# One tile of a block taken from a table held on chip by 0/1 products, in two of three blocks of the first layer and one of four of the second

## The chip, the cores and the metric

The kernel runs on one core of a Trainium2 chip. The metric is the device time of that core in microseconds (us), as the median of several runs. A difference of about 0.2% is what a measurement of this kernel can tell from no change.

## The reference

Two layers of a graph network run one after the other over 6250 nodes with 128 features and 200,000 edges, which are sorted by the node that they end at (`dst`). Cut to what matters:

```python
h = maximum(layernorm(x), 0)                       # layer 0: attention with 8 heads
z = (h @ W).reshape(N, 8, 16)
el, er = einsum(z, attn_l), einsum(z, attn_r)      # (N, 8) each
e = leaky_relu(el[src] + er[dst], 0.2)
a = exp(e - segment_max(e, dst)[dst])
agg = segment_sum(z[src] * a[:, :, None], dst)
x = x + agg / maximum(segment_sum(a, dst), 1e-9) + bias

h = maximum(layernorm(x), 0)                       # layer 1: tensor product messages
s, v = h[:, :32] @ W_up_s / sqrt(32), (h[:, 32:] by 3) @ W_up_v / sqrt(32)
w0, w1, w2, w3 = split(silu(silu(f8 @ A1 + b1) @ A2 + b2) @ A3, 4)
msg = [s[src]*y_s*w0, dot(v[src], y_v)/sqrt(3)*w3, s[src]*y_v*w1, v[src]*y_s*w2]   # 256 per edge
x = x + (segment_sum(msg, dst) / 10) @ W_out / sqrt(64)
```

All of it is in float32. What matters here is `z[src]` with `el[src]` in layer 0, and `s[src]`, `v[src]` in layer 1: for each of the 200,000 edges a row of a table is fetched, 136 floats wide in layer 0 and 128 in layer 1.

## The kernel before, in words

The edges are cut into 1563 tiles of 128 edges, one edge to a partition. 16 tiles (`KB`) make a block; there are 98 blocks (`NB`). The inputs are such that a block's edges end within 128 nodes of a window that moves on by 64 nodes from block to block (a check at the start takes another path otherwise). The nodes stand in 50 tiles of 128 (`NX`).

A first stage computes the table of layer 0 and writes it to HBM as `ft0` (in the profile `ft`). Then layer 0 goes through the blocks, and while it does so it writes the rows of the table of layer 1, `ft1` (also `ft` in the profile), as nodes become complete. Layer 1 then goes through the blocks again.

**Where the rows come from.** Most tiles are gathered: `gather` (L833) issues one indirect DMA from GpSimd (POOL) for each tile, 128 rows each, into a column of the block's tile `g`. `z_pool` holds five such tiles `g`, and `take_rows` asks for a block's rows some blocks ahead, so POOL waits only for a free `g`. In every third block (`by_row`, 31 blocks) the last tile is fetched in another way: `rows_by_row` issues 128 single-row DMAs from SyncE (SP), at L1130, to a tile `r`, with the row numbers read into registers at L1126, 32 at a time; `filled` copies `r` into `g` on ScalarE. `rows_until` spreads these row DMAs between SP's other work, some three blocks ahead of their use. The first 24 tiles of layer 1 are gathered from `ft1z`, a copy of the table in which the last three node tiles are zero, so that they can start before layer 0 ends; `late_ends` and `late_rows` add the missing rows by products.

**Layer 0**, one iteration of the loop for each block `c`, written out by hand in order for TensorE, VectorE, ScalarE and SP. `logits` (L1228) adds the gathered `el` and the `er` of the block, and TensorE transposes the sum (L1231). `ends_of` builds the 0/1 matrices `s` of the block after next (L1149); `masks_of` (L1193), `turned` (L1203, the 0/1 matrices transposed on TensorE into the bank `p_d`, of which there are two, and evicted by ScalarE) and `er_of` (L1214) prepare the next block; `maxima`, `neighbours`, `weights` finish the softmax of the block before (`exp` at L1270, and its transpose at L1271); `weighted` (L1281) scales the rows, and `sums` (L1286) adds them up by products with `s`. Each second block completes a node tile: `node_x` to `node_s` compute its `x` and its row of the next table, and `node_out` has SP write it to `ft1` and `ft1z` (L1350). `x` of all nodes stays on chip in `fx_all`. The gathers of the next blocks run beside all this on POOL.

**Layer 1**, four tiles at a time: `network` (L1568, L1572) computes the edge network of the next block, `tensor_weights` (L1585) its last product, `messages` (L1605 to L1614) multiplies on VectorE, `one_hot` (L1149) builds the 0/1 matrix, `sums1` (L1622) adds up. `node1` multiplies with `W_out` and `node_out1` writes the result (L1642). `edge_rows` has SP load a block's edge inputs (L1549, L1551).

Of the kernel before, what the change touches and what calls it, by code (L numbers as in the profile page):

```python
# [18 lines left out]
P = 128  # L19
# [722 lines left out]
def tile_even_edges(  # L742
# [88 lines left out]
    def gather(to, table, tiles, width, first=0):  # L831
        for k, t in enumerate(tiles, first):
            nc.gpsimd.indirect_dma_start(  # L833
                out=to[:, k, :width], out_offset=None, in_=table,
                in_offset=bass.IndirectOffsetOnAxis(ap=src_col[:, t : t + 1], axis=0))
        return to
# [171 lines left out]
def even_edges(tc, v):  # L1008
# [8 lines left out]
    with ExitStack() as ctx:  # L1017
        z_pool = ctx.enter_context(tc.tile_pool(name="fz", bufs=5))
        const = ctx.enter_context(tc.tile_pool(name="fconst", bufs=1))
        s_pool = ctx.enter_context(tc.tile_pool(name="fs", bufs=16))  # L1020
        row_pool = ctx.enter_context(tc.tile_pool(name="frow", bufs=3))
        of_l0 = ctx.enter_context(ExitStack())
        l0c = of_l0.enter_context(tc.tile_pool(name="l0c", bufs=1))
# [15 lines left out]
        x_all = const.tile([P, NX, P], F32, name="fx_all")  # L1039
# [3 lines left out]
        identb = l0c.tile([P, P], BF, name="fidentb")  # L1043
        nc.vector.tensor_copy(identb, ident)
# [50 lines left out]
        a3p = const.tile([P, 2, P], F32, name="fa3p")  # L1095
        nc.sync.dma_start(a3p, v["a3p"])
# [4 lines left out]
        wout = const.tile([P, 2, P], F32, name="fwout")  # L1101
        nc.sync.dma_start(wout, v["wout"])
# [5 lines left out]
        with tc.tile_pool(name="fat_ps", bufs=1, space=PSUM) as at_ps:  # L1108
            col = l0c.tile([P, P], F32, name="fcol")
# [36 lines left out]
        def one_hot(t, m, iota=iota):  # L1146

            s = s_pool.tile([P, 4, P], F32, name="s")
# [17 lines left out]

        sv_late = const.tile([P, NL, P], F32, name="fsv_late")
# [4 lines left out]
        with tc.manual_schedule(engines=in_order), \  # L1172
                tc.tile_pool(name="l0", bufs=2) as l0, \
                tc.tile_pool(name="l0n", bufs=2) as l0n, \
                tc.tile_pool(name="l0_ps", bufs=1, space=PSUM) as l0_ps:
# [5 lines left out]
            nc.scalar.copy(iota_p, iota)  # L1181

# [15 lines left out]
            def turned(c, q):  # L1198
                if 4 * q < c["kt"]:
                    m = min(4, c["kt"] - 4 * q)  # L1200
                    p_d = l0_ps.tile([P, 4, P], F32, name="p_d", bufs=2)
# [87 lines left out]

            def node_rows(i, n):  # L1290
                nc.sync.dma_start(x_all[:, i : i + n, :],
                                  xp[i * P : (i + n) * P].rearrange("(j p) f -> p j f", p=P))

            def with_bias(i, n):
                x_i = x_all[:, i : i + n, :]
                nc.vector.tensor_add(x_i, x_i, bias_b[:, None, :].to_broadcast([P, n, F]))

            def node_x(u):
                i, n, agg = u["i"], u["n"], u["agg"]
                x_i = x_all[:, i : i + n, :]  # L1300
# [14 lines left out]
            def node_h(u):  # L1315
                i, n = u["i"], u["n"]
                rs, mr = normal(l0n, u["mv"], u["rs"], n, f"n{n}")
                xn = u["xn"] = l0n.tile([P, 2, P], F32, name="xn")
                nc.scalar.activation(xn[:, 0, :], x_all[:, i, :], AF.Identity, bias=mr[:, 0, :],
                                     scale=rs[:, 0, :])  # L1320
                if n == 2:
                    nc.vector.tensor_scalar(xn[:, 1, :], x_all[:, i + 1, :], u["mv"][:, 1, 0:1],
# [20 lines left out]
            def node_out(u):  # L1343
                i, n, sv = u["i"], u["n"], u["sv"]
                first = i * P - W0
                for table in (t1, t1z) if i < LATE else (t1,):
                    if i == 0:
                        nc.sync.dma_start(table[: P - W0, :], sv[W0:, 0, :])
                    else:
                        nc.sync.dma_start(  # L1350
                            table[first : first + n * P].rearrange("(j p) f -> p j f", p=P), sv)

# [12 lines left out]
            def take_rows(g):  # L1365
                if 0 < g < NG:
                    c = cs[g]
                    t = c["b"] * KB + c["o"]
                    c["z"] = gathered(t0, range(t, t + c["kt"] - (c["b"] in by_row)), ZW)
# [42 lines left out]
            rows, rows_until.n, late = rows_by_row(0, t0, ZW), 0, []  # L1412
            for i in range(2):
                node_rows(i, 1)
            for g in range(NG - 3):
# [3 lines left out]
                for n in late:  # L1419
                    node_out(n)  # L1420
                if g % 2 == 0 and g // 2 + 2 < NX - 2:
# [6 lines left out]
                logits(c)  # L1428
                ends_of(n2, 0)
# [3 lines left out]
                maxima(c)  # L1433
                ends_of(n2, 1)
# [5 lines left out]
                er_of(n1, 0)  # L1440
                if b4:
                    weights(b4)
                for n in nodes:
# [3 lines left out]
                if b4:  # L1447
                    bank_of(b4)
                    weighted(b4, 0)
                turned(n1, 3)  # L1450
                er_of(n1, 2)
                if b4:
                    weighted(b4, 8)
                for n in nodes:
# [4 lines left out]
                if b4:  # L1459
                    sums(b4, 0)  # L1460
                for n in nodes:
# [6 lines left out]
                late = nodes  # L1468
                if b4:
                    sums(b4, 8)  # L1470
                if g == NG - 4:
# [8 lines left out]
            for n in late:  # L1480
                node_out(n)
            with_bias(NX - 2, 2)
# [5 lines left out]
            maxima(c3)  # L1488
            neighbours(c4, c5, c3)
# [26 lines left out]
            (u,) = ended(c4, st)  # L1516
            weighted(c2, 0)
# [22 lines left out]
        with tc.manual_schedule(engines=in_order), \  # L1540
                tc.tile_pool(name="l1", bufs=3) as l1, \
                tc.tile_pool(name="l1n", bufs=2) as l1n, \
                tc.tile_pool(name="l1_ps", bufs=2, space=PSUM) as l1_ps:

# [8 lines left out]
            def network(b, step):  # L1553
# [7 lines left out]
                if step == 3 or 2 * q0 + 8 >= KT[b] and second:  # L1561
                    c["yp"] = held[:, P + b % 3 * KB * 3 : P + (b % 3 + 1) * KB * 3].rearrange(
# [61 lines left out]

            def node1(i, agg):
                x_i = x_all[:, i, :]
                p_n = l1_ps.tile([P, 4, P], F32, name="p_n", bufs=1)
# [3 lines left out]
                nc.scalar.copy(m_t, p_n[:, :2])  # L1631
                for q in range(2):
                    nc.tensor.matmul(p_n[:, 2, :], m_t[:, q, :], wout[:, q, :], start=q == 0, stop=q == 1)
                nc.vector.scalar_tensor_tensor(x_i, p_n[:, 2, :], POST, x_i, op0=OP.mult, op1=OP.add)
                return i

            def node_out1(i):
                x_i = x_all[:, i, :]
                if i == 0:
                    nc.sync.dma_start(out[: P - W0, :], x_all[W0:, 0, :])  # L1640
# [5 lines left out]
            iota_p = held[:, :P]  # L1646
# [25 lines left out]
            def late_rows(t):  # L1672
                if t < NE:
                    z, k0, oh = blk[t // KB]["z"], t % KB, late_ends.of.pop(t)
                    p_n = l1_ps.tile([P, 4, P], F32, name="p_n", bufs=1)
# [224 lines left out]
```

## Time and profile before

| what | value |
|---|---|
| median of 3 runs | 3866.83 us (3866.21 to 3874.36) |
| the profiled execution's own time | 3867.01 us |
| its span in the profile | 3865.1 us |
| POOL busy | 2900.2 us (75%), of it 3024 gathers at L833 2857.7 us |
| PE (matmul) busy | 2825.6 us (73%) |
| DVE (VectorE) busy | 2237.5 us (58%) |
| ACT (ScalarE) busy | 1403.0 us (36%) |
| mean granted TensorE clock | 0.813 |

The profile tells each engine's busy time; a group of instructions has its line, engine, operation, output and input, count, busy time, mean ns of one, and the idle time of its engine before it with what ended it. A float32 product is two instructions on TensorE. The granted clock (PEclk) is the share of full speed at which TensorE runs. Layer 0's loop lasts from about 60 us to about 1960 us of the span, and layer 1's from there to the end.

### The profile page before, as it was taken

What the parts mean: (1) busy time and instruction counts of PE and PEld (TensorE: products, weight loads), DVE (VectorE), ACT (ScalarE), POOL (GpSimd) and SP (SyncE); (2) the same over time, 40 slices, a digit from 0 to 9 for tenths busy, and PEclk for the clock granted to TensorE, in tenths of its full rate; (3) what the DMA queues carried; (4) which work ended last, traced back from release to release, by engine and by line L of the source; (5) the groups of instructions that cost most, each with busy time, mean ns of one, the idle gap of its engine ahead of it and who ended that gap; (6) DMA issues with size and microseconds to landing.
All of it is one profiled execution on the core that took longest, in us unless ns stands there. A gap on an engine that the chain in (4) does not pass through costs nothing. (4 is left out here: it accounts for less than half of the span.)

```text
span 3865.1 us, 62861 instructions
## 1 busy us (share of the span) xinstructions
PE 2825.6 (73%) x14836; PEld 2380.3 (62%) x14836; DVE 2237.5 (58%) x5485; ACT 1403.0 (36%) x3625; POOL 2900.2 (75%) x3074
## 2 busy tenths in 40 slices
PE   4666566666666666666688888888887788888777
PEld 3666566666566656656576666666665666666655
DVE  6555444444444444444457777777766666666666
ACT  3333322232323233322324444444444444444443
POOL 6777777777777777777777777777777777777776
PEclk7676666666666666666689999999999999999999
DMA  6222222222222222222222222222222222222221
GB/s 176 60 64 62 65 64 62 65 64 63 63 64 63 64 62 65 62 64 62 62 60 62 62 62 62 62 63 62 61 63 62 62 62 62 62 61 62 61 61 50
DMA packets 192048, 250.91 MB, mean 65 GB/s; under 512 B 78768, under 2 KB 141872, under 8 KB 191664
## 3 DMA queue, kind: packets, MB, share of 16 engines
q0 software_dynamic: 98048, 207.21, 22.6%
q1 hardware_dynamic: 93184, 39.50, 3.9%
q8 instruction: 120, 1.97, 0.2%
q14 instruction: 264, 2.16, 0.2%
q10 hardware_dynamic: 432, 0.08, 0.0%
HBM read 232.98 MB, written 13.25 MB: 64 GB/s over the span
## 5 line engine op out<-in xcount | busy, mean ns | idle before, releaser
L833 POOL DMA_INDIRECT g<-ft,fsrc x3024 | 2857.7, 945 | 934.4 <-issue 859.1
L1622 PE MATMUL p_u<-mj,s 128*128 128x256 f32 x3126 | 793.6, 398 | 211.2 <-DVE mj L1614 209.8
L1622 PEld LDWEIGHTS p_u<-mj,s 128*128 128x128 f32 x3126 | 591.1, 196 | 379.4 <-DVE mj L1614 303.3
L1286 PE MATMUL p_u<-g,s 128*128 128x136 f32 x3062 | 588.1, 372 | 1.0 <-DVE g L1281 0.4
L1286 PEld LDWEIGHTS p_u<-g,s 128*128 128x128 f32 x3062 | 563.2, 276 | 1.7 <-DVE g L1281 1.6
L1589 ACT ACTIVATE p_w<-p_w,yb 128x64 f32<-128x64 f32 x1563 | 450.3, 288 | 120.5 <-PE p_w L1585 78.8
L1605 DVE TENSOR_TENSOR vy<-g,p_i 128x384 f32<-128x384 f32 x387 | 213.0, 550 | 364.6 <-DMA g<-ft,fsrc 258.1
L1585 PE MATMUL p_w<-fa3p,h 128*128 128x256 f32 x1564 | 412.3, 387 | 0.0
L1203 PE MATMUL p_d<-fident,s 128*128 128x128 f32 x1563 | 370.6, 400 | 0.9 <-DVE s L1149 0.9
L1585 PEld LDWEIGHTS p_w<-fa3p,h 128*128 128x128 f32 x1564 | 289.3, 195 | 117.9 <-issue 51.9
L1228 DVE TENSOR_TENSOR e_s<-g,p_n 128x128 f32<-128x128 f32 x96 | 27.5, 286 | 554.6 <-DMA g<-ft,fsrc 498.1
L1570 ACT ACTIVATE h<-p_h,fb 128x512 f32<-128x512 f32 x196 | 134.7, 687 | 580.2 <-PE p_h L1568 580.2
L1203 PEld LDWEIGHTS p_d<-fident,s 128*128 128x128 f32 x1563 | 300.7, 218 | 11.6 <-DVE s L1149 1.1
L1196 ACT COPY mk<-p_m 128x385 f32<-128x385 f32 (+1 forms) x99 | 47.7, 482 | 701.4 <-PE p_m L1193 693.6
L1281 DVE TENSOR_TENSOR g<-g,pe 128x1024 f32<-128x1024 f32 x193 | 225.5, 1209 | 127.3 <-ACT g L1272 127.3
L1205 ACT CAST d<-p_d 128x512 bf16<-128x512 f32 x391 | 228.2, 586 | 180.4 <-PE p_d L1203 137.2
L1231 PE MATMUL pe<-fident,e_s 128*128 128x128 f32 x98 | 37.7, 384 | 329.9 <-DVE e_s L1229 329.9
L1149 DVE TENSOR_TENSOR s<-p_n,fdloc 128x512 f32<-128x512 f32 x391 | 266.1, 682 | 7.2 <-ACT sv L1341 3.4
L1149 DVE TENSOR_TENSOR s<-p_i,fdloc 128x512 f32<-128x512 f32 x391 | 266.4, 681 | 3.8 <-ACT p_i L1564 3.8
L1568 PE MATMUL p_h<-ft,fa1p 128*128 128x128 f32 x1568 | 215.4, 282 | 67.7 <-DMA ft<-in_e_f_dram 67.7
L1568 PEld LDWEIGHTS p_h<-ft,fa1p 128*128 128x128 f32 x1568 | 209.2, 196 | 88.6 <-issue 72.4
L1575 ACT ACTIVATE h<-p_h,fb 128x512 f32<-128x512 f32 x196 | 134.7, 687 | 304.4 <-PE p_h L1572 304.4
(213 smaller groups left out, 3345.6 us busy)
## 6 DMA issues: line engine op xcount, KB each, us to landing
r<-ft SPq DMA_DIRECT2D x3968, 0.5 KB
r<-ft SPq DMA_DIRECT2D x3968, 0.5 KB
g<-ft,fsrc POOLq DMA_INDIRECT x3024
ft<-in_e_f_dram SPq DMA_DIRECT2D x98, 64.0 KB
yb<-in_e_y_dram SPq DMA_DIRECT2D x98, 32.0 KB
fx_all<-in_e_xp_dram SPq DMA_DIRECT2D x48, 64.0 KB
out_dram<-fx_all SPq DMA_DIRECT2D x47, 64.0 KB
ft<-sv SPq DMA_DIRECT2D x46, 64.0 KB
```

The source lines that it names most:

```text
L833: nc.gpsimd.indirect_dma_start(out=to[:, k, :width], out_offset=None, in_=table, in_offset=bass.IndirectOffsetOnAxis(ap=src_col[:, t : t + ...
L1149: nc.vector.tensor_tensor(s[:, :m], iota[:, None, :].to_broadcast([P, m, P]), dloc[:, t : t + m].unsqueeze(2).to_broadcast([P, m, P]), OP. ...
L1203: nc.tensor.transpose(p_d[:, k, :], c["s"][q][:, k, :], ident)
L1205: nc.scalar.copy(d[:, :m], p_d[:, :m])
L1281: nc.vector.tensor_mul(zh, zh, p_a[:, k0 : k0 + m].unsqueeze(3).to_broadcast([P, m, H, D]))
L1286: nc.tensor.matmul(c["p_u"][:, :ZW], c["s"][k // 4][:, k % 4, :], c["z"][:, k, :], start=c["o"] + k == 0, stop=c["o"] + k == KT[c["b"]] - 1)
L1568: nc.tensor.matmul(p_h[:, q, :], a1p[:, q0 + q, :], c["ft"], start=True, stop=True)
L1570: nc.scalar.activation(c["h1"], p_h, AF.Silu, bias=b1)
L1585: nc.tensor.matmul(w[:, k : k + n].rearrange("p k a u -> p (k a u)"), c["h2"][q // 4][:, q % 4, :], a3p[:, :n].rearrange("p k f -> p (k f) ...
L1589: nc.scalar.activation(w[:, k, ::2, :], w[:, k, ::2, :], AF.Copy, scale=c["yb"][:, k0 + k, 0:1])
L1605: nc.vector.tensor_mul(vy, v_n, y_p)
L1622: nc.tensor.matmul(blk[b]["p_u"][:, :MW], u["s"][:, k, :], u["mj"][:, k, :], start=k0 + k == 0, stop=k0 + k == KT[b] - 1)
```

## The change

In 48 blocks of layer 0 (set `dense`: from block 21 to 93, those not in `by_row`) and in 21 blocks of layer 1 (`dense1`: every fourth from block 10), one tile of the block (`KD`, the last but one) is no longer gathered. Its rows come from products with the whole table, which is held on chip as the sum of three bfloat16 parts (`t0s`, `t1s`; `in_three` splits a float32 into them).

The 50 node tiles are taken in three ranges of 17, 17 and 16, so one 0/1 matrix of 128 by 128 serves three node tiles at once. For a tile of edges, `spread` (`dense_ends` in layer 1) turns its 128 node numbers, reduced to a place within their range (`key`), into a row on every partition by one product; `ends_to` compares it with the places of 17 node tiles, in two VectorE instructions, to 17 bfloat16 0/1 matrices; `rows_of` (`dense_rows`) makes 17 times 3 bfloat16 products, each 408 columns wide in layer 0 and 384 in layer 1, that add up in one bank `p_x`; and `taken` (`dense_taken`) picks of the three ranges the right one with `part`, in three VectorE instructions, into `g`.

In layer 0 the table is read back from HBM in the first 17 iterations (`asked`, one SP transfer of three node tiles) and split (`split`). In layer 1 the parts come ready: layer 0 splits each node tile of the new table (`parts`) and writes `x` and the parts together to a new HBM tensor `fx1` (`parts_out`, one SP transfer of 128 by 320 floats a node tile), and layer 1 loads them in its first eight blocks (`table_tiles`). `x` no longer stays on chip: layer 1 reads it back from `fx1` (`node_rows1`), one transfer a node tile. To make room in PSUM, `p_d` has one bank where it had two (the other is `p_x`). The weights `fa3p` and `fwout` are loaded where layer 1 begins, not in the setup; the order on SP there is: the write of the last but two node tiles' table rows, their `x`, `fa3p`, `fwout`, five loads of edge inputs, then the write of the last two tiles' table rows.

The counts on the engines as the built programs have them: POOL's gathers go from 1516 to 1468 in layer 0 and from 1508 to 1487 in layer 1 (from `ft1`); TensorE gets 3519 products and as many weight loads of the new kind, and 69 spreads; SP gets 47 writes of `fx1` with parts and 2 without, 49 reads of `x` from it, 8 loads of `t1s` and 18 reads of the table.

```diff
         def gather(to, table, tiles, width, first=0):
-        for k, t in enumerate(tiles, first):
+        for t in tiles:
+            k = first + t - tiles[0]
...
+        NR = -(-NX // 3)
+        KD = KB - 2
+        order = sorted(range(NR), key=lambda k: (k > 0, 2 * NR + k < NX, k))
+        half = (NR + 1) // 2
+        TS = 3
+        dense = {b for b in range(-(-NX // TS) + 4, NB - 4) if b not in by_row}
+        dense1 = set(range(10, NB - 4, 4))
...
+        def in_three(to, of, rest):
+            to = [to[..., k, :] for k in range(3)]
+            nc.vector.tensor_copy(to[0], of)
+            nc.vector.tensor_sub(rest, of, to[0])
+            nc.vector.tensor_copy(to[1], rest)
+            nc.vector.tensor_sub(to[2], rest, to[1])
...
+            def spread(c, pe):
+                b = c["b"]
+                c["at"] = pe[:, 2 * P : 3 * P]
+                nc.tensor.matmul(c["at"], ranges[0][:, b : b + 1].to_broadcast([P, P]), ident,
+                                 start=True, stop=True)
+            def ends_to(c, h):
+                n = half if h == 0 else NR - half
+                oh = c["oh", h] = ohs[:, h * half : (h + 1) * half, :]
+                nc.vector.tensor_tensor(
+                    oh[:, :n], c["at"].unsqueeze(1).to_broadcast([P, n, P]),
+                    ranges[2][:, h * half : h * half + n].unsqueeze(2).to_broadcast([P, n, P]), OP.is_equal)
+            def rows_of(c, k0, n):
+                if k0 == 0:
+                    p_x = l0_ps.tile([P, 512], F32, name="p_x")
+                    c["p_x"] = p_x[:, : 3 * ZW].rearrange("p (r f) -> p r f", f=ZW)
+                for k in range(k0, min(k0 + n, NR)):
+                    i = order[k]
+                    m = len(range(i, NX, NR))
+                    for s in range(3):
+                        nc.tensor.matmul(c["p_x"][:, :m, :], c["oh", k // half][:, k % half, :],
+                                         t0s[:, i::NR, s, :], start=k == 0 and s == 0,
+                                         stop=k == NR - 1 and s == 2)
+            def taken(c):
+                b, z, part = c["b"], c["z"][:, KD, :], ranges[1]
+                nc.vector.tensor_scalar(z, c["p_x"][:, 0, :], part[:, b, 0:1], None, op0=OP.mult)
+                for r in (1, 2):
+                    nc.vector.scalar_tensor_tensor(z, c["p_x"][:, r, :], part[:, b, r : r + 1], z,
+                                                   op0=OP.mult, op1=OP.add)
...
-                    p_d = l0_ps.tile([P, 4, P], F32, name="p_d", bufs=2)
+                    p_d = l0_ps.tile([P, 4, P], F32, name="p_d")
...
-                    c["z"] = gathered(t0, range(t, t + c["kt"] - (c["b"] in by_row)), ZW)
+                    c["z"] = gathered(t0, [k for k in range(t, t + c["kt"])
+                                           if not (c["b"] in by_row and k % KB == KB - 1)
+                                           and not (c["b"] in dense and k % KB == KD)], ZW)
...
                 logits(c)
+                to, was = n2["b"] in dense, n1["b"] in dense
+                if to:
+                    spread(n2, c["pe"])
                 ends_of(n2, 0)
                 if n1 is not none:
                     masks_of(n1)
                 turned(n1, 0)
                 maxima(c)
+                if to:
+                    ends_to(n2, 0)
+                if was:
+                    rows_of(n1, half, 4)
+                for n in late:
+                    parts(n)
                 ends_of(n2, 1)
...
                 er_of(n1, 0)
+                if was:
+                    rows_of(n1, half + 4, NR)
                 if b4:
                     weights(b4)
+                if was:
+                    taken(n1)
...
                     weighted(b4, 0)
+                if to:
+                    ends_to(n2, 1)
                 turned(n1, 3)
                 er_of(n1, 2)
                 if b4:
                     weighted(b4, 8)
+                if to:
+                    rows_of(n2, 0, 3)
...
                     sums(b4, 0)
+                if to:
+                    rows_of(n2, 3, 3)
...
                     sums(b4, 8)
+                if to:
+                    rows_of(n2, 6, half - 6)
+                split(g - 3)
...
+            def dense_step(b, q):
+                if b + 1 in dense1:
+                    if q == 1:
+                        dense_ends(b + 1)
+                    elif q > 1:
+                        dense_rows(b + 1, (q - 2) * 4, 4)
+                if b in dense1:
+                    dense_rows(b, 8 + 3 * q, 3)
+                    if q == 2:
+                        dense_taken(b)
```

## The prediction

> **What bounds the kernel now.** I read the busy row of the page, then the groups, the chain of waits, the windows by stage, and the timeline of single iterations. First POOL:
>
> ```profile
> L833 POOL DMA_INDIRECT g<-ft,fsrc x3024 | 2857.7, 945 | 934.4 <-issue 859.1
> POOL g L833 <- issue: 861.0, 2823, 0.3
> DVE e_s L1228 <- DMA g<-ft,fsrc: 500.2, 81, 12.0
> DVE vy L1605 <- DMA g<-ft,fsrc: 258.1, 159, 3.7
> ...
> 1200.00:1700.00 500.00, 332.58 (x1959) 304.91 (x1960) 231.25 (x505) 153.16 (x347) 377.90 (x401) 0.65 0.28 63
> 2200.00:2700.00 500.00, 418.47 (x1925) 330.98 (x1926) 355.41 (x907) 219.24 (x617) 377.99 (x401) 0.97 0.24 62
> ```
>
> The first row gives 75% busy, but the idle time before a gather is 0.30 us each and called issue: POOL waits for nobody. 401 gathers in 500 us, in both layers: one per 1.249 us (0.945 plus 0.30), from 60 us to the end. VectorE waits for landed rows in both layers. So the time is the number of gathers times 1.249 us plus a head and a tail, as long as the other engines keep pace. The two window rows (columns: length, PE, PEld, DVE, ACT, POOL busy, clock, DMA) show what room they have: PE 66% at a granted clock of 0.65 in layer 0, 84% at 0.97 in layer 1.
>
> One iteration of layer 0, and what the clock does in it:
>
> ```profile
> 1220.05 0.29 DVE L1228 TENSOR_TENSOR e_s<-g,p_n 128x128 f32<-128x128 f32 x1 [4.58 <-DMA g<-ft,fsrc]
> 1227.24 0.47 PE L1271 MATMUL pe<-fident,a 128*128 128x128 f32 x1 [2.25 <-ACT a L1270]
> 1230.47 5.55 PE L1286 MATMUL p_u<-g,s 128*128 128x136 f32 x32
> 1239.66 0.29 DVE L1228 TENSOR_TENSOR e_s<-g,p_n 128x128 f32<-128x128 f32 x1 [7.27 <-DMA g<-ft,fsrc]
> ...
> 1232.00:1233.00 1.00, 1.00 (x6) 1.00 (x6) 0.40 (x1) 0.00 (x0) 0.81 (x1) 0.50 0.29 72
> 1234.00:1235.00 1.00, 1.00 (x11) 1.00 (x10) 0.00 (x0) 0.00 (x0) 0.69 (x2) 1.00 0.30 66
> 1241.00:1242.00 1.00, 1.00 (x7) 1.00 (x6) 0.97 (x3) 0.48 (x1) 0.69 (x2) 0.50 0.31 72
> ```
>
> It starts when rows land (1220.05), PE ends it at 1236.0, and the next rows come at 1239.66: 16.0 us of work in a period of 19.6. An iteration with a node tile (1201.07 to 1217.9) takes 16.9. The clock is 0.50 through most of it, becomes 1.00 after 3 us of unbroken sums, and falls back after the idle stretch.
>
> The queue next to its limit is SP's:
>
> ```profile
> 1217.51 0.42 SPq L1291 DMA_DIRECT2D fx_all<-in_e_xp_dram  x1
> 1218.03 34.57 SPq L1130 DMA_DIRECT2D r<-ft  x84
> ```
>
> A row DMA comes each 0.32 us, and 32 of them need a register load of 2.17 us (L1126). A third of 128 rows a block is 42.7 x 0.32 = 13.7 us, loads 1.33 x 2.23 = 3.0, the node transfers (0.43 + 0.47 + 0.50)/2 = 0.7: 17.4 us of 19.6.
>
> **The change, part by part.** *Gathers removed.* 48 in layer 0 and 21 in layer 1: 69 x 1.249 = 86.2 us less on POOL. Three blocks of layer 0 took 47 gathers = 58.7 us and will take 45 = 56.2; four of layer 1 went from 78.1 to 76.9. This is the whole gain; the rest asks whether the others keep this pace.
>
> *TensorE in layer 0.* No product like the new ones is in the loop. The nearest rows: four bf16 products of the setup (L923, three of 512 columns) start 0.215 us apart at full clock, 0.42 ns a column, so 408 columns take 0.171 us, and 0.34 at half clock (the 385-column L1193 there keeps PE 0.32). Their weight load (bf16, L1214: 0.18 us for four at full clock, 0.42 at half) is shorter and lies beside. A dense block has 51, a pair of dense blocks 102 in three iterations: 17.4 us at full clock, 34.7 at half. The old work of one iteration at full clock, from the warm rows at 1920: transposes and masks 0.8, four `turned` at 0.64 = 2.6, neighbours 1.0, four `er_of` at 0.26 = 1.0, sums 2 x 2.02 = 4.0: 9.4, so 28.2 for three; with 0.8 for nodes and 0.6 for two spreads, PE has 47.0 of 56.2 us, 84%, the share at which layer 1 runs now. Waits add: the one for `exp` (2.25) is filled by 12 products where the block is followed by a dense one, so once in three: 2.3. One bank `p_d` makes the fourth transpose wait for the eviction of the third (0.59 plus two hops of 0.1): 0.8 x 3 = 2.4. Nodes 0.8, small gaps 1.0. Sum 53.5 us, 2.7 under the gathers.
>
> Here a rule decides, so row and rule are weighed. By the mean clock of the window (0.65) a product is 0.26 and the old PE work 13.3 an iteration: 102 x 0.26 + 40 = 66.5 us before any wait, 8 over today's 58.7. The Trainium skill (TensorE: Matmul & The Clock Gate, What's actually happening) says that the gate has two states only and opens after about 3.4 us of sustained activity, and closes after an idle window; the three clock rows agree (0.50, 1.00, 0.50). Twelve products in a row are 4.1 us at half clock, so a dense iteration opens it early, and work at 95% of the period leaves no idle window to close it. I take full clock, 53.5, and keep 66.5 as the other end. A closed gate at the start of every third iteration costs 3.5 us, but it needs idle time to close, so it appears only when there is time to spare.
>
> *VectorE.* `ends_to` 9 and 8 x 128 elements: L1149 takes 0.68 for 512, so 1.35 and 1.2; `taken` 3 x 0.29. 3.4 us a dense block, on an engine with 9 of 19.6 us in use: hidden by PE's longer order. In layer 1 it has 355 of 500 us; 3.5 more in four blocks, hidden.
>
> *The splits and POOL.* `in_three` runs 17 times on 408 columns and 47 on 128: by L998 and L999 casts 0.37 and subtractions 0.58, at 128 columns 0.23 and 0.29. As VectorE work it is covered (1.9 us an iteration, early). But:
>
> ```profile
> 54.49 1.89 DVE L1067 TENSOR_TENSOR feq<-fd_q 128x1664 f32<-128x1664 int32 x1 [10.42 <-DMA fd_q<-in_e_dstt_dram]
> 54.63 2.56 POOL L833 DMA_INDIRECT g<-ft,fsrc  x1 [0.30 <-issue]
> ```
>
> a gather beside a long two-input VectorE instruction took 2.56 us, not 0.94. The skill (SBUF — State Buffer, Who interferes with whom) speaks against this change: casts and copies in a two-port mode lock GpSimd out for their whole length, and so do two SBUF inputs against GpSimd's reads. By the rule each of the 256 instructions could cost POOL its own length: 34 x (0.37 + 0.58) + 94 x (0.23 + 0.29) = 81 us, nearly the whole gain. By the rows, the 144 short two-input instructions of the nodes (L1296, L1308, L1309, 0.29 each) do not show: the pitch is 1.249 in both layers. I take 2 us, for the 408-column ones.
>
> *SP.* One `fx1` write for each second block (by L1291 0.5, so 0.25) and one read of the table in 17 blocks (0.5): layer 0 asks 17.7 us a block, 18.2 at first, of 18.7. Layer 1: 13.7 + 3.0 + edge loads 0.95 + output 0.25 = 17.9, plus 0.25 for reading `x` back = 18.1, of 19.3 on average. Eight loads of `t1s` are 590 KB each; the nearest (fxs, 384 KB) took 1.0 us to issue; if the rows behind wait for landing, 3 us more. Behind SP's waiting transfers stand the row DMAs, for which ScalarE's copy and `logits` wait. In layer 1 the gathers of block 7 begin 22.6 us after block 2's last messages (counted in the timeline), which covers that. SP is within its room by 0.5 to 1.2 us a block.
>
> *TensorE in layer 1.* A step of four tiles takes 3.49 us (2520.56 to 2524.05); with nodes 14.9 a block, 59.4 for four; 51 x 0.161 and a spread add 8.4: 68 of 76.9. Covered.
>
> *The seam.*
>
> ```profile
> 1962.15 0.43 SPq L1350 DMA_DIRECT2D ft<-fsv_late  x1
> 1967.45 0.94 POOL L833 DMA_INDIRECT g<-ft,fsrc  x1 [0.30 <-issue]
> ```
>
> The last write of the table is issued 5.3 us before the first gather that needs it; with 2.6 us to issue and land (a gather's rows come 2.2 us after its end), 2.7 are free. The change puts about 6 transfers of 0.45 in front of that write, 2.9 us, and parts of 1.0 us into VectorE's tail: I book 2 us.
>
> Sum against the profiled execution's 3867.0 us (its span 3865.1 and 1.9 around it; the median shown is 3866.8, the same): 3867.0 - 86.2 + 2 + 2 = 3785.
>
> **The rivals.**
> *Part of the gain is lost to SP or to the splits (3800 to 3858, middle 3825).* If a big transfer holds SP's rows back by 0.7 us a block, layer 0 asks 19.2 of 18.7: 73 x 0.5 = 35 us late, of which blocks 94 to 97 (16 gathers, 16.5 us of work) win back 14; layer 1 similarly 20. For it: SP has no idle in the timeline of 1218 to 1253. Against: it can lose only what the pace has gained.
> *TensorE becomes the bound of layer 0 (slower).* Place: the 24 triples of iterations in the dense blocks. Up to 56.8 us a triple nothing is lost (14 us are won back at the end); each us beyond costs 24, so it decides at 56.8 + 82/24 = 60.2 us. At 63 (gate closed for a third of it) the time is 3785 + 149 = 3934; at 66.5, 4018. For it: the order is strict, products stand ahead of `neighbours` and of the transpose of `a`, and the clock is 0.50 there today. Against: layer 1 holds 0.97 at 84%.
> *The change does not remove the gathers*: excluded, the built order has 69 fewer.
>
> **How the numbers follow.** All kept, 3779 to 3800: 0.58. Part lost, 3800 to 3858: 0.23. Within 0.2% (3859 to 3874.5; about what a measurement of this kernel can tell from no change): 0.05. PE the bound, slower: 0.14. The likeliest is 3785; the range 3779 to 3858 holds the first two cases, 0.81. Faster 0.81, same 0.05, slower 0.14.
>
> **What would show it.** Right: 2955 gathers from `ft`, with 0.30 of issue before nearly all; a granted clock of 0.9 or more between 500 and 1850 us, PE above 80% there; VectorE still waiting for landed rows at L1228's successor. SP wrong: ScalarE waits for `r` throughout. Splits wrong: many gathers over 1.0 us in the first 400 us. PE wrong: POOL waits for `sums` (a free `g`), and the clock stays near 0.65.

## The result and the profile after

The changed kernel takes 3804.4 us (median of 4 runs, 3804.2 to 3812.9), the kernel before on the same chip 3866.5 us: a ratio of 0.984 (95% interval 0.982 to 0.986). That is faster, by 62 us, where 82 were forecast (3785). The profiled execution spans 3802.4 us, against 3865.1.

The groups of the page after, POOL's gathers and the new products of layer 0 (count, then busy time and mean ns, then idle time before and what ended most of it):

```profile
L834 POOL DMA_INDIRECT g<-ft,fsrc x2955 | 2793.9, 945 | 936.3 <-issue 840.8
L1284 PE MATMUL p_x<-t0s,fz_first 128*128 128x408 bf16 (+1 forms) x2448 | 480.9, 347 | 0.0
```

69 gathers fewer, each of the same 945 ns. Now the stages (columns: length, PE, PEld, DVE, ACT and POOL busy, clock, DMA share, GB/s):

```profile
1000.00:1500.00 500.00, 402.59 (x3012) 313.56 (x3010) 314.08 (x668) 159.06 (x359) 378.04 (x401) 0.92 0.30 68
2200.00:2700.00 500.00, 456.39 (x2274) 354.31 (x2274) 373.86 (x927) 218.02 (x610) 377.69 (x402) 1.00 0.25 64
```

POOL still starts 401 gathers in 500 us in both layers. So in the steady state every removed gather is worth its 1.249 us, and TensorE, at 81% and 91%, keeps pace. What is missing must be a place. The waits of the whole run (total us, times, longest) show it:

```profile
POOL g L834 <- issue: 843.2, 2765, 0.3
DVE t0s L1207 <- DMA zr<-ft: 74.6, 14, 32.1
POOL g L834 <- DVE part L1191: 21.8, 1, 21.8
DVE e_s L1340 <- DMA g<-ft,fsrc: 11.0, 11, 1.3
POOL g L834 <- DMA ft<-fsv_late: 1.8, 1, 1.8
```

One wait of POOL of 21.8 us, once. And VectorE waits 32.1 us for a read of the table (`zr`). Both stand in the timeline around 180 us, here SP's queue, VectorE, TensorE and POOL (start, length, instruction, idle time before it and what ended it):

```profile
178.75 0.33 SPq L1241 DMA_DIRECT2D zr<-ft  x1
180.16 4.82 SPq L1133 DMA_DIRECT2D r<-ft  x15
...
149.05 0.69 DVE L1152 TENSOR_TENSOR s<-p_n,fdloc 128x512 f32<-128x512 f32 x1
181.86 0.58 DVE L1207 CAST t0s<-zr 128x408 bf16<-128x408 f32 x1 [32.12 <-DMA zr<-ft]
184.21 0.28 DVE L1340 TENSOR_TENSOR e_s<-g,p_n 128x128 f32<-128x128 f32 x1
...
195.54 6.28 PE L1398 MATMUL p_u<-g,s 128*128 128x136 f32 x32
...
179.86 0.94 POOL L834 DMA_INDIRECT g<-ft,fsrc  x1 [0.30 <-issue]
202.59 0.94 POOL L834 DMA_INDIRECT g<-ft,fsrc  x1 [21.79 <-DVE part L1191]
```

Read it in order of time. VectorE ends its work of iteration 3 at 149.7 and comes to the first `split`. The read for it is issued by SP at 178.75 only: SP could begin the row DMAs of layer 0 only at 85 us, has 152 of them (59 us) ahead of anything else in its order, and is behind from then on. The logits of block 4 stand behind the split in VectorE's order and start at 184.21. In the run without the wait (below) they start at 153.0. The sums that free the `g` of block 3 (L1398) end at 201.8. That is the `g` that block 8 needs, the fifth after it, so POOL, which was some 60 us ahead of the logits, stands from 180.8 to 202.59. The row names `part` (L1191) because this was the last VectorE instruction to end before. But POOL starts 0.77 us after the end of the sums, and at the stops of two other runs below (with a tile by products in every third block of layer 1, and without any in layer 1) it is again 0.76 to 0.77 us, with another instruction of VectorE named, or none. So POOL waited for the sums, and what made them late was the split.

### The profile page after: what moved, and what is told of

Same layout as the page of the kernel before. It is cut to its first block, busy times and chain, and to the rows that moved or that the text cites. A ratio compares the mean times of both kernels' runs of the same rounds, so it can differ in the third digit from the quotient of the medians.

```text
span 3802.4 us, 70869 instructions
## 1 busy us (share of the span) xinstructions
PE 3117.4 (82%) x18493; PEld 2470.2 (65%) x18493; DVE 2557.8 (67%) x6114; ACT 1409.7 (37%) x3625; POOL 2836.4 (75%) x3005
## 3 DMA queue, kind: packets, MB, share of 16 engines
q0 software_dynamic: 95840, 202.48, 22.5%
## 5 line engine op out<-in xcount | busy, mean ns | idle before, releaser
L834 POOL DMA_INDIRECT g<-ft,fsrc x2955 | 2793.9, 945 | 936.3 <-issue 840.8
L1793 PE MATMUL p_u<-mj,s 128*128 128x256 f32 x3126 | 762.0, 387 | 86.9 <-DVE mj L1785 84.8
L1793 PEld LDWEIGHTS p_u<-mj,s 128*128 128x128 f32 x3126 | 580.3, 192 | 214.2 <-DVE mj L1785 137.6
L1398 PE MATMUL p_u<-g,s 128*128 128x136 f32 x3062 | 476.2, 320 | 18.5 <-DVE g L1393 18.5
L1284 PE MATMUL p_x<-t0s,fz_first 128*128 128x408 bf16 (+1 forms) x2448 | 480.9, 347 | 0.0
L1398 PEld LDWEIGHTS p_u<-g,s 128*128 128x128 f32 x3062 | 451.7, 226 | 22.8 <-DVE g L1393 21.0
L1315 PE MATMUL p_d<-fident,s 128*128 128x128 f32 x1563 | 297.3, 322 | 71.8 <-ACT d L1317 70.2
L1284 PEld LDWEIGHTS <-fz_first 128*128 128x128 bf16 x2448 | 240.8, 101 | 155.9 <-issue 17.2
L1315 PEld LDWEIGHTS p_d<-fident,s 128*128 128x128 f32 x1563 | 213.7, 168 | 106.4 <-ACT d L1317 99.8
L1393 DVE TENSOR_TENSOR g<-g,pe 128x1024 f32<-128x1024 f32 x193 | 229.1, 1207 | 61.9 <-ACT g L1384 56.2
L1739 PE MATMUL p_h<-ft,fa1p 128*128 128x128 f32 x1568 | 215.5, 282 | 60.2 <-DMA ft<-in_e_f_dram 60.2
```

The lines of the kernel that those rows point to most:

```text
L834: nc.gpsimd.indirect_dma_start(out=to[:, k, :width], out_offset=None, in_=table, in_offset=bass.IndirectOffsetOnAxis(ap=src_col[:, t : t + ...
L1284: nc.tensor.matmul(c["p_x"][:, :m, :], c["oh", k // half][:, k % half, :], t0s[:, i::NR, s, :], start=k == 0 and s == 0, stop=k == NR - 1 ...
L1315: nc.tensor.transpose(p_d[:, k, :], c["s"][q][:, k, :], ident)
L1393: nc.vector.tensor_mul(zh, zh, p_a[:, k0 : k0 + m].unsqueeze(3).to_broadcast([P, m, H, D]))
L1398: nc.tensor.matmul(c["p_u"][:, :ZW], c["s"][k // 4][:, k % 4, :], c["z"][:, k, :], start=c["o"] + k == 0, stop=c["o"] + k == KT[c["b"]] - 1)
L1739: nc.tensor.matmul(p_h[:, q, :], a1p[:, q0 + q, :], c["ft"], start=True, stop=True)
```

## The experiments

Differences to the kernel before are given as ratios of the same chip's runs, since chips differ (before: 3867.6 to 3874.1 us in the runs below, unless said otherwise). In the six runs marked as of other chips the kernel before itself took 6293 to 6316 us, so their ratios can't be set beside the others.

### The wait taken away, the work kept

```diff
-                    zr = asked.of.pop(k)
+                    asked.of.pop(k)
...
-                    in_three(t0s[:, TS * k : TS * k + n], zr, rest0[:, :n])
+                    in_three(t0s[:, TS * k : TS * k + n], z_first[:, 13 : 13 + n, :], rest0[:, :n])
```

> The table reads stay on SP as they are, but the splits take their values from an old tile of the same shape and not from the read (so the table of layer 0 held on chip is not the right one; the work on every engine is the same). Only VectorE's wait for the read is gone. Theory (the wait): 3783 us (3780 to 3788), no POOL gap over 3 us near 180 us. Rival A (the splits' work or the port): 3804, the gap stays. Rival B (the reads hold up SP's row DMAs): 3804, VectorE and ScalarE wait for r instead.

The table held on chip is not the right one here, but each engine has the same instructions. Measured: 3789.3 us against 3874.1, ratio 0.978 (0.977 to 0.979): 85 us less, where the change itself brings 62. The expected 3780 to 3788 us are 0.978 to 0.980 of the first chip's time, so the theory held. POOL's largest row of waits:

```profile
POOL g L834 <- issue: 834.9, 2736, 0.3
```

and its timeline where the stall was:

```profile
180.06 0.95 POOL L834 DMA_INDIRECT g<-ft,fsrc  x1 [0.30 <-issue]
181.31 0.94 POOL L834 DMA_INDIRECT g<-ft,fsrc  x1 [0.30 <-issue]
```

The same reads, casts and subtractions, and no POOL wait over 0.3 us in the loops. So the 21.5 us were the wait for the read. Neither the splits' work nor the reads' load on SP made them. The small wait at the seam (1.8 us for the table's last write, in the waits of the changed kernel) is gone too. Whether it came of the stall is not shown: the run without layer 1's products (below) has the stall and not this wait.

### The reads from ScalarE

```diff
-                        nc.sync.dma_start(zr, of.rearrange("(j p) f -> p j f", p=P))
+                        nc.scalar.dma_start(zr, of.rearrange("(j p) f -> p j f", p=P))
```

(and the two reads of the first three tiles alike)

> The 18 reads of the layer 0 table (zr) are issued by ScalarE instead of SP; nothing else changes. Theory (the 21.5 us between the forecast and the result are one POOL stall at 180 us, which comes from VectorE waiting at the first split for a table read that stands behind SP's late row DMAs): the gap of 22.7 us between two gathers is gone or under 3 us, 3804.4 - 21.5 = 3783 us (3780 to 3788). Rival A (the splits' own VectorE time, or casts that hold POOL's port): the work stays, so the gap stays, 3804. Rival B (one bank p_d and the products pace TensorE, the stall is only where it shows first): the loss appears elsewhere, 3800 to 3805.

Measured: 3854.2 us (six runs, 3840.8 to 3856.2), ratio 0.994 (0.992 to 0.995). No expectation was right: most of the change's gain was lost again. POOL stands 5 to 11.5 us in six places before 510 us, and 5.7 and 8.0 us at the seam. The waits of SP's queue and of ScalarE:

```profile
SPq L1133 <- DMA zr<-ft: 86.1, 9, 18.1
...
ACT g L1147 <- DMA r<-ft: 111.0, 26, 23.9
```

and ScalarE's timeline where it issues the second read:

```profile
152.61 0.31 ACT L1147 COPY g<-r 128x136 f32<-128x136 f32 x1 [23.87 <-DMA r<-ft]
152.62 0.38 ACTq L1246 DMA_DIRECT2D zr<-ft  x1
```

SP's row DMAs now wait for the reads, though they share no data. The built program gives a reason: the transfers of both queues take eight completion counters in turn, in the order of the program, and a transfer waits for the last one on its counter. That SP's waits are these is read from it; the trace names only the read. The read that ScalarE has to issue stands behind ScalarE's copy of `r` (152.61, then 152.62), the copy waits for SP's rows, and SP's rows wait for an earlier read. With all transfers on SP such a wait was over before it was met (0.5 us in all between 60 and 420 us of the changed kernel). So a transfer that is moved to another queue to get past a late one can tie the two queues together.

### SP given less to do at the start

```diff
-            for b in by_row:
+            for b in by_row[1 - layer :]:
...
-            if b in by_row:
+            if (layer, b) in rows_by_row.tiles:
...
-                                           if not (c["b"] in by_row and k % KB == KB - 1)
+                                           if not (c["b"] in by_row[1:] and k % KB == KB - 1)
...
-            rows, rows_until.n, late, split_ = rows_by_row(0, t0, ZW), 0, [], []
+            rows, rows_until.n, late, split_ = rows_by_row(0, t0, ZW), 32, [], []
```

> In layer 0 the last tile of block 3 is gathered like the others, so SP's 128 row DMAs and 4 register loads of that block (about 45 us of its queue at the start) are gone and everything behind them, the table reads too, is issued that much earlier. The reads keep their place in SP's order, one iteration before their split. Theory (VectorE waits because SP is late, not because the read is long): the first read is issued near 135 us instead of 179, VectorE does not wait for it, no POOL gap over 3 us near 180 us, one gather more: 62.1 + 21.5 - 1.2 = 82 us less than before, ratio 0.9787 (0.977 to 0.981). Rival (the read, wherever it stands, holds the row DMAs or VectorE up): 0.984 as the changed kernel, or worse.

(`rows_until.n` starts at 32 groups of four, so the pacing counts the 128 rows as issued.) Measured: 3783.1 us against 3867.6, ratio 0.978 (0.977 to 0.980): 84 us less, as the theory had it. This version beats both kernels. SP's queue in the timeline:

```profile
126.83 0.33 SPq L1241 DMA_DIRECT2D zr<-ft  x1
```

and the waits of VectorE and POOL:

```profile
POOL g L834 <- issue: 837.0, 2745, 0.3
DVE e_s L1340 <- DMA g<-ft,fsrc: 89.7, 48, 7.1
...
DVE t0s L1207 <- DMA zr<-ft: 6.9, 3, 5.4
```

The first read is issued at 126.8 instead of 178.75, in the same place of SP's order. The split waits 5.4 us at most, where it waited 32.1. It costs one gather and brings back the whole stall. So VectorE waited because SP was late. And VectorE waits for landed rows again (89.7 us; 500.2 before the change, 11.0 in the changed kernel): the other engines have caught up with the gathers.

### One layer at a time

```diff
-        dense = {b for b in range(-(-NX // TS) + 4, NB - 4) if b not in by_row}
+        dense = set()
...
-                asked(g - 2)
...
-                split(g - 3)
```

> Layer 0 without dense blocks, without the table reads and splits; layer 1 keeps its 21 dense blocks and p_d keeps one bank. Theory: 48 gathers come back, +60.0 us, and the stall of 21.5 us and about 1 us of stretched gathers go: 3804.4 + 60.0 - 22.5 = 3842 us (3838 to 3846); no long POOL gap. Rival (the loss is not from reads and splits but from the single p_d bank or from the parts and fx1 writes): 3861 to 3865.

Measured: 3848.3 us, ratio 0.9934 (0.992 to 0.995), 26 us less than before, as expected: layer 1's 21 gathers are worth 26.2. No stall in layer 0, so neither the single bank `p_d` nor the writes of `fx1` cost time that could be seen (the interval is 5 us to either side). The run without the wait lies 59.0 us under this one, and 48 gathers are 60.0: reads, splits and products cost POOL about 1 us together.

```diff
-        dense1 = set(range(10, NB - 4, 4))
+        dense1 = set()
```

> Layer 1 without dense blocks (the parts are still written to fx1 and loaded); layer 0 as in the changed kernel. Theory: 21 gathers come back at 1.249 us, all of them on the path: 3804.4 + 26.2 = 3830.6 us (3828 to 3833). Rival (layer 1's gain was partly lost to the loads of t1s or to TensorE): a smaller step, 3815 to 3827.

Measured: 3837.4 us, ratio 0.990 (0.989 to 0.992), 37 us less than before, as expected; with the change's 62, from another chip, that makes 25 for layer 1, against 26.2. The stall stands where it was, as POOL's longest wait in the loops:

```profile
POOL g L834 <- DVE key L1189: 22.3, 1, 22.3
```

### The reads one iteration earlier, and more tiles in layer 1

```diff
-            rest0 = l0d.tile([P, TS, ZW], F32, name="rest0")
+            rest0 = z_first[:, KB - TS :, :]
...
-                    zr = asked.of[k] = l0d.tile([P, TS, ZW], F32, name="zr", bufs=2)[:, :n]
+                    zr = asked.of[k] = l0d.tile([P, TS, ZW], F32, name="zr", bufs=3)[:, :n]
...
-                asked(g - 2)
+                asked(g - 1)
...
-        dense1 = set(range(10, NB - 4, 4))
+        dense1 = set(range(10, NB - 4, 3))
```

> The reads of the table one iteration earlier on SP, with three buffers zr, and a tile by products in every third block of layer 1 (28 instead of 21). Theory: POOL's stall near 180 us shrinks from 21.8 to about 2 us (20 less), and 7 gathers of 1.249 us go (8.7 less): 62 + 20 + 9 = 91 us less than before, ratio 0.9765. Rival A (the splits themselves, not the wait): the stall stays, 0.982. Rival B (TensorE cannot keep pace in layer 1): POOL waits for sums1 after 1960 us, 0.979 or more.

Measured: 3836.0 us, ratio 0.991 (0.989 to 0.992): 37 us less than before, and about 25 more than the change alone. In layer 0 the theory held in the main: the first read is issued at 159.8, VectorE's longest wait for one is 13.5 us (the row below), and POOL stands 4.1 and 2.5 us near 180 and 203 instead of once 21.8 (2 were expected).

```profile
DVE t0s L1207 <- DMA zr<-ft: 57.7, 14, 13.5
```

The last gather in the timeline, and a window of the end (columns as before):

```profile
3768.73 0.95 POOL L834 DMA_INDIRECT g<-ft,fsrc  x1 [0.30 <-issue]
```

```profile
3700.00:3800.00 100.00, 91.42 (x444) 71.72 (x445) 74.66 (x189) 44.14 (x124) 52.90 (x56) 0.98 0.16 47
```

In layer 1 rival B was right, in another form: the last gather starts at 3768.7, some 19 us earlier than in the changed kernel, and the span ends at 3835.7, 66 us after it instead of 14. TensorE, 91% busy, still works off what the gathers left behind. (It does not stand for want of edge inputs from SP: its waits for these are 22.8 us in the whole run, 60.2 in the changed kernel.) The products trail the gathers by 45.2 us at block 13 and by 56.0 at block 91 (start of a block's messages minus the end of its last gather, counted in the timeline): 0.42 us more in each three blocks, so three blocks take 57.5 + 0.4 = 57.9 us, where the forecast's terms give 53. POOL waits no longer than 1.0 us there, since five `g` buffers hold the trail; the loss shows at the end alone. With every fourth block the trail shrinks, if slowly: from 40.7 us at block 12 to nothing only at block 72 (in the run without the wait).

### Six runs on other chips

The earlier reads with a tile by products in every fourth, third and second block of layer 1, and with every fourth and a fourth product for each 0/1 matrix of layer 0 (the cut shows the line of that last one):

```diff
-                    for s in range(3):
+                    for j, s in enumerate((0, 1, 2, 2)):
...
```

> The reads of the table stay on SP but stand one iteration earlier in its order (asked(g - 1)), into three buffers zr instead of two; the place for the third is won by letting the splits' remainder use an old tile. Theory (the wait of the first split for the read): a read is issued about 20 us earlier (near 160 us instead of 179), VectorE waits about 12 us instead of 32, POOL's stall of 21.8 us shrinks to 2 (the five g buffers took up the other 10 us of the 32 before): 82 us less than before, ratio 0.979 (0.977 to 0.981). Rival (the splits' work, or SP's total load): as the changed kernel, 0.984.

> As the earlier asking, and layer 1 takes a tile by products in every third block (28 blocks) instead of every fourth (21). Theory (layer 1 is worth 1.249 us a removed gather as long as TensorE keeps pace; it has 3 x 14.9 + 8.4 = 53 us of work in 57.5): 7 x 1.249 = 8.7 us less than the earlier asking alone, ratio 0.9765. Rival (TensorE or its late start after the seam bounds layer 1 already): no gain, or slower by up to 20 us, with POOL waiting for sums1.

> As the earlier asking, with every second block of layer 1 (42 blocks). If TensorE kept pace: 21 x 1.249 = 26.2 us less than the earlier asking alone, ratio 0.972. Theory: TensorE has 2 x 14.9 + 8.4 = 38.2 us of work for 37.9 us of gathers and cannot win back the 40 us by which the products trail the gathers after the seam, so POOL waits for free g buffers early in layer 1 and throughout: slower than with every third block, 0.977 to 0.985. This shows where the price of a tile in TensorE's time ends the gain.

> As the earlier asking, but each 0/1 matrix of layer 0 is multiplied with four parts instead of three (the last part is added twice, so the rows differ in their last bits): 34 products more in three blocks, 5.8 us at full clock. It measures how far TensorE was from being the bound of layer 0. By the forecast's 53.5 us a triple: 59.3 of 56.8, 24 x 2.5 = 60 us more than with three parts, and POOL waits for sums. Rival (TensorE is already at 56 us a triple, since the products trail the gathers by 25 us for 60 blocks): 120 us more. Rival (SP sets that trail and TensorE has more room than booked): under 20 us.

The kernel before took 6315.8 us there. Measured ratios: 1.049 (1.047 to 1.051), 1.057 (1.055 to 1.059), 1.060 (1.058 to 1.062) and 1.062 (1.060 to 1.065), in this order. Two of them were run once more and came to another such chip (before: 6292.5 us):

> The reads of the table one iteration earlier on SP, with three buffers zr, and a tile by products in every third block of layer 1 (28 instead of 21). Theory: POOL's stall near 180 us shrinks from 21.8 to about 2 us (20 less), and 7 gathers of 1.249 us go (8.7 less): 62 + 20 + 9 = 91 us less than before, ratio 0.9765. Rival A (the splits themselves, not the wait): the stall stays, 0.982. Rival B (TensorE cannot keep pace in layer 1): POOL waits for sums1 after 1960 us, 0.979 or more. On a chip where SP's row DMAs take 0.6 us each instead of 0.32, SP sets the time and the run tells nothing of these.

> The earlier reads, layer 1 as in the changed kernel, and each 0/1 matrix of layer 0 multiplied with four parts instead of three (the last part is added twice, so the rows differ in their last bits): 34 products more in three blocks, 5.9 us at the measured 0.173 us. It measures how far TensorE's order was from being the bound of layer 0. By the forecast's 53.5 us a triple: 59.4 of 56.8, 24 x 2.6 = 62 us more than with three parts, ratio 0.995. Rival (TensorE's order is already at 56 us, since the products trail the gathers by a constant 11 to 25 us): 24 x 5.1 = 122 us more, ratio 1.010. Rival (more room than booked): under 20 us, ratio under 0.984.

Measured: 1.060 (1.058 to 1.061) and 1.064 (1.062 to 1.066). The waits of the first of the six:

```profile
ACT h L1746 <- remote: 688.0, 65, 15.4
ACT d L1317 <- remote: 655.2, 103, 13.2
```

ScalarE stands still for 6 to 11 us at a time on average in these two rows and up to 22.5 in others, and the profile names no engine or transfer of this program for it ("remote"). It is not ScalarE alone: VectorE has such stops of up to 16.5 us, and POOL pauses of up to 16.2 us for which nothing is named. POOL's gathers keep their mean of 947 ns, but POOL is idle for 3639 us before them. SP stops as well (40 row DMAs took 29.3 us from 702.5 on, 15.6 near there in the run without the wait), so the slower pace of its row DMAs, which an expectation takes for the cause, may be a consequence. None of the expectations can be judged. What can be said: on those chips, where the gathers are not the bound, the change with the earlier reads is a loss of some 5%, and the versions with more products lose more. The changed kernel as it stands was not run there. What makes those chips stand still stays open, and so does how many products more layer 0 would have borne on the others, which the fourth part was to measure.

## Why the prediction was right, and where it was 20 us off

*Right in what bounds the kernel.* The measured 3804.4 us lie in the range (3779 to 3858), but 4 us outside its likeliest part (3779 to 3800). The mechanism held: with the wait alone taken away, the ratio is 0.978, and 3785 of 3867 is 0.979. POOL's pitch stayed 1.249 us, and both layers' gathers were worth what they were booked at: 59.0 for 60.0 and 25 to 26 for 26.2. By the trace the sum now closes: 86.2 of gathers, less 21.5 for the stall (21.8 less the usual 0.3), 1.5 at the seam (2 booked) and 1.4 for all gathers' mean, which rose by half a nanosecond (2 booked): 61.8, against 62.7 between the spans. So the terms of the forecast were right within a microsecond, but for one that it put at nothing.

*The step that failed:* "As VectorE work it is covered (1.9 us an iteration, early)." The splits' work was covered, and the added wait was not counted. The prediction costed the read by SP's rate ("18.2 at first, of 18.7") and found room. It did not ask when SP reaches it. The kernel before shows that. Just ahead of SP's transfer of `x` in iteration 2 the first read was put, and SP comes to it at 179.68; its split was put just ahead of the logits of block 4, which VectorE begins at 151.59:

```profile
179.68 0.37 SPq L1291 DMA_DIRECT2D fx_all<-in_e_xp_dram  x1
151.59 0.29 DVE L1228 TENSOR_TENSOR e_s<-g,p_n 128x128 f32<-128x128 f32 x1 [0.91 <-ACT sv L1341]
```

So SP was 28 us late for it before anything was changed, and an instruction on an in-order engine with one iteration between asking and using inherits that. What was hidden behind SP's lateness became a stop of VectorE, then of the sums, then, with five `g` filled, of POOL. The rival "part of the gain is lost to SP or to the splits" names the time (3800 to 3858) but not the form: not 0.7 us a block, but one stop of 22 us.

*The rule on ports, weighed rightly.* By the prediction's sum from the Trainium skill (SBUF — State Buffer, Who interferes with whom) the 256 instructions of the splits could have locked POOL out for up to 81 us. The run that keeps them all and drops the wait is 85 us faster than before. Casts of 0.58 us (0.37 booked) and of 0.21 to 0.23 us cost POOL about 1 us in all. This does not refute the rule: it speaks of casts in a two-port mode, and the casts of 408 columns took as long as the subtractions of as many (0.58 us), so that they ran in such a mode is not shown. Longer ones were not tried.

*TensorE in layer 0: right side, thinner room.* Forecast 53.5 us of 56.2 a triple. In 1200 to 1256.2 PE is busy 47.5 us (47.0 booked). It waits 3.9 for `exp` (2.3 booked), 2.2 for `p_d` (2.4) and 1.8 in the node's turn (0.8). After the stall, the logits trail the gathers by 22.6 us at block 21 and 23.5 at block 60: they win back next to nothing in 13 triples, so the triple takes close to 56. With the earlier reads the same triples win back 0.8 us each (23.3 us at block 21, 12.7 at block 60). Either way the room was under 1 us, not 2.7. The clock stands at 1.00 where products are dense, as forecast, but closes sooner than the forecast had it (windows of the changed kernel, columns as above):

```profile
1216.00:1219.00 3.00, 0.39 (x7) 0.28 (x5) 2.86 (x9) 1.17 (x4) 2.39 (x3) 0.75 0.30 67
1219.00:1222.00 3.00, 2.22 (x13) 1.76 (x14) 2.86 (x7) 0.85 (x2) 2.08 (x4) 0.50 0.23 51
1225.00:1228.00 3.00, 3.00 (x24) 2.46 (x24) 0.69 (x2) 0.49 (x1) 2.33 (x3) 1.00 0.46 116
```

In the one iteration of three whose next block has no products, PE waits 2.7 us for `exp`. The clock falls to 0.50 some 1.1 us into this wait, at 1217.5, and is back at 1.00 near 1224.3, with the next block's products. In the 3.4 us before it fell PE was busy 2.1. That is the "closed gate at the start of every third iteration", named in the forecast and left out of the sum because work at 95% "leaves no idle window to close it": it closed with little time to spare, after 1.1 us of idling. The other end, 66.5 us at a mean clock of 0.65, is far from the measured 0.92. The forecast's sign that VectorE still waits for landed rows failed in the changed kernel (11.0 us in all) and held once the stall was away.

*TensorE in layer 1: right side, and SP's room was smaller than booked.* While the trail shrinks, four blocks with one tile by products take 74.3 us: 53.4 us are won back in 20 fours (block 12 to 92, run without the wait), 2.7 of 77.0 each. But this is SP's pace, not TensorE's. Without any products in layer 1 four blocks take the same, 74.0 (trail 40.4 us at block 12, 2.2 at block 48). In all these runs SP issues a block's edge inputs every 18.5 to 18.6 us (counted between 2200 and 2830), four in 74 to 75. SP itself waits for nothing longer than 0.6 us there, and TensorE waits for what SP loads. Its waits in the whole runs:

```profile
PE p_h L1739 <- DMA ft<-in_e_f_dram: 60.2, 38, 5.8
PE p_h L1739 <- DMA ft<-in_e_f_dram: 110.8, 42, 5.4
PE p_h L1739 <- DMA ft<-in_e_f_dram: 22.8, 8, 5.3
```

(the changed kernel, the run without products in layer 1, and the run with every third block). So the forecast's 68 us for TensorE in four blocks is neither shown nor refuted; SP's 18.1 us a block was 0.5 low. With every third block SP would allow 55.8 us for three blocks. They took 57.9, and there TensorE, which hardly waits for SP, is the bound: 53 were booked, 5 us too few.

*SP* was within its room in the steady state, as forecast, in layer 1 by 0.7 us of 19.25: no row of POOL's waits after the stall is over 1.8 us. *The seam* cost 1.5 us in the changed kernel and nothing in the two runs that bring the stall to an end; its cause is not shown.

## What to carry to other kernels

An added transfer has a rate and a place. When it is put behind work on a queue, look when that queue reaches it in the old trace (here 28 us after it was needed), not only whether the queue has time to spare, and give the wait for it as much distance as the queue is late. Late at the start is late for everything behind, so taking early work off the queue can be worth more than the gather that it costs. And a resource that a change fills to nine tenths gives the next step of the same change no gain: look at the tail after the bound's last instruction, because deep buffers hide that it has become the bound.

## What the runs showed of the hardware that was not expected

The same gather is 945 to 947 ns long on all chips, but on two of them ScalarE, VectorE and GpSimd stood for 15 us and more at a time without a releaser in the program, and the kernel before took 63% longer. TensorE's clock dropped to 0.50 1.1 us into a wait of 2.7 us, with 2.1 us of work in the 3.4 us before. And two queues that share no data held each other up, for 86 us; by the built program, through their completion counters.
